# Sharing the last half product of two feed-forwards, folding the layer norm's affine into weights, and a new issue order, in a fused recurrence-and-transformer kernel

## The chip, the core and the metric

The kernel runs on one core of one Trainium2 chip. The metric is device time in microseconds (us) for one execution, smaller is better. The time of a kernel is the median of several runs; a separate profiled execution supplies the trace.

## What is computed

The input `x` has 16 sequences of 512 tokens with 128 channels, all in 32-bit floats. Two branches read the normalised input and meet at the end:

```python
xn = layernorm(x)
s = recurrence(xn)                  # conv of 4 taps, two gates, a scan over time, a projection, an rms norm
t = xn
for l in range(2):                  # two transformer layers
    h = shift_token(t)              # the second 64 channels one token late
    q, k, v = split(h @ wqkv[l])    # 8 heads of 64
    t = t + local_attention(rotary(l2norm(q) * qs[l]), rotary(l2norm(k) * ks[l]), v) @ wo[l]   # windows of 64
    h = layernorm(shift_token(t)) * ln_g[l] + ln_b[l]
    a, g = split(h @ w1[l] + b1[l]) # 341 columns each
    t = t + (a * gelu(g)) @ w2[l] + b2[l]
out = x + s * silu(t)
```

The part that the change is mostly about is the last three lines of the layer: a layer norm with gain and shift, a product to 2 x 341 columns, a gated product, and a product back to 128 channels.

## The kernel before

**Work and tiles.** A sequence is 4 token tiles of 128. Per layer and tile there are three projections (`Q`, `K`, `V`), transposes of queries and keys (`tr`), scores (`sim`), a softmax (`nmA/B`, `exA/B`, `rA/B`, `PA/B`), transposes of the weights (`PT`) and the mix with the values (`PV`); per pair of tiles an output projection (`wo`). Per layer and sequence follow the layer norm and the feed-forward: `tx` transposes the stream to tokens, `bn` and `ag` take mean and variance on VectorE, `pw` raises the variance to -1/2 on GpSimd, `nm` normalises on VectorE, `th` transposes back on TensorE and `hT` copies the result to memory on ScalarE, applying gain and shift there. Then for each of three chunks of 128 columns: `g` and `a` are products on TensorE, `ge` is the GELU on ScalarE, `hi` is `(a + b) * gelu` on VectorE, and `yy` adds the chunk's product with `w2` into one accumulator. `r0` and `r1` add the result to the stream.

**Halves.** Every product with 512 columns of moving data is issued by `matmul` (L599 to L602) as two halves of 64 output columns, one for each half of TensorE's columns, and the profile counts two instructions for each half, so a product is a group "x4" there.

The feed-forward's 341 columns are padded with zeros to 384, which is 3 products for `g` and 3 for `a`, or 12 halves.

**Order.** Nothing decides the order at run time. Each task is a name and an item (a sequence, a tile or a chunk), `PLACES` gives its place in one list of 6176 tasks, `in_order` sorts them, and a loop issues them; every engine runs its own instructions strictly in this order. `OPENED` gives for each task the one of 7 accumulator banks (PSUM) that each of its tiles takes; an eighth bank holds the small norms of the attention. `ROOM` gives the number of buffers of each tile in memory. Set-up work (loads of weights, the decay rate, the rotary tables, the masks) hangs behind a few tasks in a table `behind`; for instance the decay rate, 18 small VectorE instructions, comes right behind the first sequence's statistics:

```python
        ("fbn", 0): [decay_rate], ("c0", 0): [lambda: rotary_table(0, nc.vector)],
```

**Names and lines of the profile that matter below.** L547 and L551 are statistics, L478 to L491 the decay rate, L557 to L561 the power on GpSimd, L567 and L573 the normalisation (first norm and layers' norms), L590 and L597 transposes, L602 every product made by `matmul` (`q`, `k`, `v`, `0g`, `0a`, `0y`, ..., and the taps `cv`), L611 and L613 the two copies that form the shifted stream `xS`, L617 the copy `xp`, L704 and L741 the rotary sum and the normalisation of queries and keys on GpSimd, L816 the exponentials, L830 the softmax's division on GpSimd, L851 the mix, L869 the output projection, L876 its sum, L882 `hT`, L889 the GELU, L893 `hi`, L904 `r0` and `r1`.

Of the kernel before, what the change touches and what calls it, by code (L numbers as in the profile page):

```python
# [17 lines left out]
P = 128  # L18
HEADS = 8
DH = 64  # L20
# [9 lines left out]
BANKS = 7  # L30

ROOM = {
    "0mv": 4, "1mv": 4, "fmv": 3, "g": 2, "gelu": 3, "h": 1, "hT": 2, "hid": 3, "kT": 4, "lx": 1, "max": 8, "ms": 3,
    "nx": 2, "oT": 2, "pT": 2, "pr": 3, "qT": 2, "rot": 4, "s": 4, "sq": 2, "sw": 4, "th": 3, "thi": 2, "thr": 2,
# [4 lines left out]
    "ld": "0 1 8 9 88 90 156 39 1028 170 297 535 460 331 210 576",  # L39
    "fbn": "2 2 13 85 107 45 130 25 1069 135 304 531 465 360 168 612",  # L40
    "fag": "3 3 14 97 97 61 152 49 1034 204 207 601 533 236 156 620",
    "fpw": "5 2 15 100 95 74 139 51 1032 204 208 599 699 97 148 695",
    "fnm": "8 7 26 146 156 42 1026 172 295 533 464 329 212 571 334 181",
    "ftx": "10 16 35 251 48 1006 200 299 436 519 376 205 547 349 192 511",
    "xp": "11 24 49 236 44 1005 203 298 435 522 372 208 547 353 192 506",
    "xs0": "12 19 45 254 40 1002 207 297 431 528 379 207 531 351 191 513",
    "xs1": "16 23 106 461 -181 971 276 376 426 441 426 225 456 362 167 643",
    "c0": "13 52 78 195 30 1018 195 294 434 548 351 203 561 340 193 508",
    "cv": "14 48 38",
    "c1": "21 57 69 216 15 1014 192 295 433 555 348 199 561 340 198 509",  # L50
    "c3": "25 64 68 218 13 1014 195 295 427 557 365 188 562 332 208 520",
    "gr": "42 52 214 143 128 847 263 217 442 536 363 225 528 368 208 499",
    "sr": "52 51 230 130 128 846 260 217 466 517 367 220 530 361 223 482",
    "gi": "74 46 77 221 59 958 182 295 430 553 359 194 559 350 179 530",
    "si": "87 38 91 216 75 933 183 300 429 547 367 189 576 332 181 530",
    "ea": "68 42 243 307 390 414 338 156 793 170 372 625 259 214 549 312",
    "in": "113 17 173 134 151 857 182 303 455 525 359 193 575 333 191 520",
    "a2": "86 62 214 321 376 421 341 152 858 152 314 637 250 276 487 336",
    "m": "155 126 126 319 339 475 319 147 945 65 335 802 52 290 476 333",
    "rt": "255 34 191 453 558 170 440 240 701 15 699 412 361 227 448 459",  # L60
    "u": "282 24 241 399 556 174 446 229 699 10 709 406 372 226 458 438",
    "sc": "294 19 261 420 518 174 478 194 698 40 718 365 376 225 464 453",
    "yo": "301 25 283 390 530 175 515 150 698 166 625 350 355 241 461 487",
    "s2": "307 30 280 403 514 177 514 153 706 154 626 387 319 240 459 489",
    "ms": "310 31 293 390 513 182 508 159 702 157 622 391 316 240 460 494",
    "mp": "314 32 315 367 513 184 507 159 701 157 623 389 320 237 458 496",
    "ss": "329 21 319 378 506 178 508 165 700 149 629 403 301 237 461 495",
    "c2": "371 11 1013 192 296 432 556 361 186 562 340 199 526",
    "Q": "19 10 20 36 29 36 41 27 43 177 87 59 81 89 85 69 131 63 86 54 170 60 136 40 146 107 115 44 118 103 118 67 "
    "97 68 112 58 156 57 125 46 180 88 86 69 83 62 126 31 145 143 115 81 121 79 98 22 106 134 118 47 80 137 101 42 "  # L70
    "-5045 39 80 51 133 42 91 58 139 57 95 82 137 47 150 114 135 49 101 76 160 64 103 39 133 43 102 39 187 55 123 124 "
    "144 50 84 70 119 51 115 62 218 33 96 106 141 50 99 42 189 60 80 60 161 52 93 73 200 5 27 11 99 4 47 39",
    "sqq": "24 10 32 32 30 37 56 32 23 180 74 73 88 78 87 65 132 70 76 55 192 41 133 64 117 127 108 45 136 79 114 62 "
    "105 74 117 42 157 73 111 46 192 78 84 70 100 43 138 22 144 142 108 86 123 83 89 28 115 125 118 42 94 129 99 42 "
    "-5032 38 72 52 128 49 91 53 149 41 93 86 133 72 134 113 132 46 122 60 167 59 102 64 106 45 110 40 185 67 106 126 "
    "140 47 97 60 119 60 120 62 208 31 88 117 139 39 110 39 206 35 90 82 132 67 95 72 194 2 16 21 99 3 49 38",
    "rq1": "30 10 20 32 79 15 18 36 45 164 89 58 90 74 90 64 142 52 99 43 177 57 146 43 134 106 109 47 135 89 123 61 "
    "96 66 125 42 167 56 118 45 181 98 102 44 94 57 123 39 133 152 116 83 119 72 97 31 114 113 116 60 89 116 103 75 "
    "-5079 44 81 46 131 50 86 58 147 58 89 85 135 57 152 116 123 56 96 97 135 61 98 42 133 43 102 43 182 66 117 126 "
    "142 66 98 39 117 51 115 71 208 64 73 98 143 59 86 58 175 78 61 86 140 47 96 82 185 11 27 21 85 5 50 72",  # L80
    "rq2": "27 30 16 48 53 9 24 21 71 147 88 58 89 76 96 65 144 58 84 43 177 58 142 31 150 106 109 52 120 97 133 58 "
    "90 74 105 66 159 51 119 58 191 67 111 43 102 43 138 19 149 153 110 81 126 66 95 27 105 135 115 54 81 131 119 44 "
    "-5063 35 82 66 119 49 89 51 144 61 91 88 134 52 140 132 113 61 96 111 120 62 105 49 120 43 114 29 187 84 93 149 "
    "121 64 80 70 106 64 109 72 201 37 99 108 139 50 95 42 185 77 69 63 154 62 81 82 194 3 35 7 98 6 49 73",
    "addq": "43 24 12 52 53 21 31 133 12 88 106 67 89 49 113 92 84 70 97 116 105 95 86 106 83 93 124 122 70 66 137 "
    "45 99 95 100 140 71 110 68 38 208 70 108 42 115 30 131 29 200 84 113 89 119 83 85 33 176 46 118 57 94 140 92 123 "
    "-5140 39 105 41 124 38 120 24 164 47 111 102 110 144 44 146 101 111 58 95 123 48 122 64 103 30 110 65 161 74 113 "
    "166 98 59 109 65 100 37 150 37 198 83 90 153 64 53 105 38 197 88 32 136 82 67 96 163 88 7 100 -5 40 34 50 91",
    "K": "23 10 23 34 45 24 49 17 40 177 103 53 98 60 109 54 136 52 88 50 184 48 137 38 182 90 94 66 102 101 131 53 "
    "103 73 119 39 179 38 120 65 164 95 80 77 74 78 113 48 125 143 136 66 124 69 95 41 90 136 125 42 79 132 113 33 "  # L90
    "-5037 35 89 51 124 44 82 70 125 63 98 81 137 68 127 109 137 48 110 74 171 47 106 48 120 44 107 50 175 53 121 128 "
    "153 37 85 90 110 41 114 62 219 31 118 105 127 43 99 74 166 51 80 63 158 51 101 68 196 6 52 20 74 22 25 39",
    "sqk": "28 10 37 22 61 21 47 24 36 180 97 45 120 40 114 58 140 45 85 55 186 35 139 58 164 97 80 69 109 92 137 48 "
    "107 72 121 32 186 33 127 69 160 87 86 78 81 76 110 38 145 130 136 68 116 69 98 43 101 132 116 38 81 137 110 31 "
    "-5039 40 95 63 106 43 94 61 139 66 91 64 154 50 137 119 123 63 106 59 183 60 92 49 113 55 102 38 185 59 107 126 "
    "163 32 90 86 106 54 112 64 211 33 124 90 129 55 95 73 161 47 84 79 138 56 102 78 187 11 61 15 63 25 25 29",
    "rk1": "44 7 32 44 41 -4 51 45 17 208 67 67 83 85 87 52 146 42 87 52 188 58 122 41 191 82 92 63 118 90 127 74 95 "
    "69 119 63 145 44 119 77 150 101 72 78 77 77 109 50 158 107 138 80 118 66 97 52 81 136 123 42 87 118 122 29 -5037 "
    "49 70 63 120 59 58 87 119 92 66 80 141 80 102 125 124 49 112 81 217 -5 107 62 100 55 93 58 173 49 135 119 151 74 "
    "49 98 108 52 98 75 201 53 102 124 107 73 82 61 169 69 70 71 142 62 97 65 182 24 49 26 56 20 27 43",  # L100
    "rk2": "37 17 16 53 38 37 22 32 19 182 102 67 87 81 82 59 144 37 101 43 183 61 118 47 179 90 98 60 106 102 128 "
    "63 110 64 110 63 155 46 120 62 155 110 69 79 80 68 113 52 125 139 133 90 119 62 85 57 79 137 119 47 98 112 110 "
    "45 -5046 30 90 62 115 69 64 72 129 64 82 98 130 64 124 110 147 40 106 99 191 3 107 50 126 65 78 61 161 56 115 "
    "138 146 79 58 90 111 48 99 75 217 14 125 107 136 28 99 70 164 72 82 50 152 48 110 69 197 -3 58 23 61 24 28 46",
    "addk": "48 10 35 44 63 11 18 129 16 126 86 42 116 115 51 43 135 31 96 62 171 109 72 108 157 46 100 77 123 96 "
# [174 lines left out]
}  # L280

OPENED = {
    "ftx": "01565121510532425006352661604304",
    "c0": "2431121055464",
    "cv": "202",
    "gr": "3562365444046040",
# [34 lines left out]
def all_tasks(B, NT):  # L321
# [49 lines left out]
    for s in range(B):  # L371
        add(s, ("tf", [*two("tf", s), ("th", s)]), "tn", "z", ("xld", [("x", s)]), "zs", "zx", "ot")
# [676 lines left out]
```

## Time and profile before

| what | value |
|---|---|
| runs | 1306.75, 1307.97 and 1308.43 us; median 1307.97 us |
| the profiled execution's own time | 1309.2 us |
| its span, first to last instruction | 1307.4 us, so 1.8 us lie around it |
| mean granted TensorE clock | 0.993 |
| HBM | 13.05 MB read, 4.19 MB written, 13 GB/s over the span |
| DMA issues | 224 copies `vl<-vs` (2.3 us to landing), 16 each of `xtok`, `x` and `out`, and the weights |
| ScalarE table loads | 74 of 1283 ns |

The page of the profile gives busy times of the engines (PE is TensorE's products, PEld its weight loads, DVE VectorE, ACT ScalarE, POOL GpSimd), the span in 40 slices, and the costliest groups of instructions: line, engine, operation, written and read tile, shapes and count, then busy us and mean ns of one, then the idle time just before and what ended it. Tables by stretch give the busy us of each engine between two times. The ends of products are modelled, so a group's mean duration is longer than the spacing of its instructions.

### The profile page before, as it was taken

How to read it: one execution, taken by the hardware profiler on the slowest of the kernel's cores; microseconds unless marked ns; L12 is line 12 of the kernel's file. 1: busy time of each engine (PE TensorE's matmuls, PEld its weight loads, DVE VectorE, ACT ScalarE, POOL GpSimd, SP SyncE). 2: the span in 40 equal slices, each digit the busy share in tenths (PEclk: the TensorE clock that was granted, in tenths of full speed). 3: DMA queues.
4: the chain of work that ended last, by engine and by line, in shares of the span. 5: the costliest groups of instructions: out<-in, count | busy, mean ns of one | idle time of the engine just before them, and what ended most of it. 6: DMA issues, size and time to landing. Idle time of an engine off the chain costs nothing.

```text
span 1307.4 us, 45281 instructions
## 1 busy us (share of the span) xinstructions
PE 1259.8 (96%) x17688; PEld 701.5 (54%) x17688; DVE 1132.1 (87%) x3024; ACT 1179.1 (90%) x3804; POOL 1040.1 (80%) x1009
## 2 busy tenths in 40 slices
PE   6889999999999999999999999999998999999997
PEld 2455565645555555555555555655455555655463
DVE  7989989988989989988998999879988889858963
ACT  5898999989999998998989999998999899997793
POOL 6987988966988878887877988857797698874782
PEclk9989999999999999999999999999999999999999
DMA  5110121102111202011121101211012011130111
GB/s 178 43 36 20 22 43 30 27 2 58 35 50 39 52 13 50 8 41 43 38 54 30 26 16 37 55 23 38 26 31 47 18 35 34 27 71 2 38 35 45
DMA packets 46773, 49.52 MB, mean 38 GB/s; under 512 B 4704, under 2 KB 31456, under 8 KB 46560
## 3 DMA queue, kind: packets, MB, share of 16 engines
q1 hardware_dynamic: 46560, 46.63, 14.6%
q8 instruction: 140, 2.29, 0.7%
q14 instruction: 73, 0.60, 0.2%
HBM read 13.05 MB, written 4.19 MB: 13 GB/s over the span
## 4 chain that ended last, share of the span: by engine, by line
PE 53%; DVE 19%; ACT 16%; POOL 8%; issue 4%; DMA 0%; POOLq 0%; DVEq 0%; ACTq 0%
ACT pr L816 6%; PE q L602 5%; PE x L869 5%; PE o L851 5%; PE sA L803 5%; PE k L602 5%; PE t L762 4%; PE v L602 3%; PE p L838 3%; DVE xn L573 3%; PE 0y L602 3%; PE 1g L602 3%; PE 0a L602 3%; DVE rot L697 2%; DVE norms L709 2%
## 5 line engine op out<-in xcount | busy, mean ns | idle before, releaser
L704 POOL TENSOR_TENSOR rot<-rot,sw 128x512 f32<-128x512 f32 x256 | 326.9, 1290 | 35.2 <-DVE rot L697 12.2
L830 POOL TENSOR_TENSOR pr<-pr,sum 128x512 f32<-128x512 f32 x256 | 263.7, 1042 | 93.0 <-DVE sum L824 65.3
L741 POOL TENSOR_TENSOR rot<-rot,y 128x1024 f32<-128x1024 f32 x128 | 242.9, 1903 | 38.5 <-DVE y L736 37.1
L816 ACT ACTIVATE pr<-sA,max 128x128 f32<-128x128 f32 x512 | 189.0, 441 | 4.4 <-DVE max L809 3.3
L816 ACT ACTIVATE pr<-sB,max 128x128 f32<-128x128 f32 x512 | 188.6, 442 | 1.4 <-DVE max L809 1.1
L709 DVE TENSOR_REDUCE norms<-sq 128x16 f32<-128x1024 f32 x128 | 155.7, 1217 | 6.1 <-ACT sq L690 4.2
L842 ACT COPY pT<-p 128x512 f32<-128x512 f32 x256 | 143.6, 657 | 14.9 <-PE p L838 14.4
L851 PEld LDWEIGHTS o<-pT,vl 128*64 128x64 f32 x2048 | 111.4, 138 | 49.1 <-issue 29.1
L816 ACT ACTIVATION_READ_ACCUMULATOR pr<-sB,max 128x1 f32 x512 | 137.8, 281 | 0.0
L816 ACT ACTIVATION_READ_ACCUMULATOR pr<-sA,max 128x1 f32 x512 | 137.6, 280 | 0.0
L602 PE MATMUL q<-wqkv,xS 128*64 128x512 f32 x512 | 135.3, 611 | 0.5 <-ACT pr L816 0.2
L803 PE MATMUL sA<-kT,qT 64*64 64x128 f32 x2048 | 134.8, 270 | 0.0
L803 PE MATMUL sB<-kT,qT 64*64 64x128 f32 x2048 | 134.2, 270 | 0.0
L602 PE MATMUL k<-wqkv,xS 128*64 128x512 f32 x512 | 133.7, 604 | 0.5 <-ACT pr L816 0.5
L602 PE MATMUL v<-wqkv,xS 128*64 128x512 f32 x512 | 132.3, 600 | 1.5 <-DVE rot L697 0.6
L851 PE MATMUL o<-pT,vl 128*64 128x64 f32 x2048 | 128.2, 224 | 0.9 <-ACT pr L816 0.5
L851 PE MATMUL o<-pT,vs 128*64 128x64 f32 x2048 | 126.9, 223 | 0.0
L803 PEld LDWEIGHTS sA<-kT,qT 64*64 64x64 f32 x2048 | 121.2, 134 | 8.9 <-issue 0.2
L869 PE MATMUL x<-oT,wo 128*64 128x257 f32 x1024 | 123.1, 382 | 0.0
L803 PEld LDWEIGHTS sB<-kT,qT 64*64 64x64 f32 x2048 | 120.6, 134 | 0.0
L851 PEld LDWEIGHTS o<-pT,vs 128*64 128x64 f32 x2048 | 105.0, 139 | 0.2 <-ACT pT L842 0.2
L809 DVE TENSOR_REDUCE max<-sA 128x4 f32<-128x512 f32 x128 | 87.0, 680 | 16.2 <-PE sB L803 14.6
(155 smaller groups left out, 3218.3 us busy)
## 6 DMA issues: line engine op xcount, KB each, us to landing
vl<-vs SPq DMA_DIRECT2D x224, 128.0 KB, 2.3
xtok<-in_x SPq DMA_DIRECT2D x16, 256.0 KB, 3.1
x<-in_x SPq DMA_DIRECT2D x16, 256.0 KB, 3.4
out<-th SPq DMA_DIRECT2D x16, 256.0 KB, 2.4
wqkv<-in_wqkv SPq DMA_DIRECT2D x2, 768.0 KB, 6.8
w<-in_w SPq DMA_DIRECT2D x2, 384.0 KB, 6.3
rot<-in_rope SPq DMA_DIRECT2D x1, 512.0 KB, 5.8
wo<-in_wo SPq DMA_DIRECT2D x2, 256.0 KB, 5.2
```

Source lines behind the costliest of these rows:

```text
L602: nc.tensor.matmul(ps[col : col + 64], w[:, col : col + 64], v, start=start, stop=stop)
L704: nc.gpsimd.tensor_tensor(r, r, at["sw", *n, "qk"[i]], ALU.add)
L709: nc.vector.tensor_reduce(at["nx", *pair(n)][:, 0, 16 * j : 16 * j + 16], sq, AX.X, ALU.add)
L741: nc.gpsimd.tensor_tensor(flat, flat, bc(at["y", *pair(n)][:, 0, 16 * j : 16 * j + 16], DH), ALU.mult)
L762: nc.tensor.transpose(four(at["bank", f"t{w}", *n])[:, i, p, :], r[rows, i, 2 * p : 2 * p + 2, :], c["ident"][rows, rows])
L803: nc.tensor.matmul(out_(w, par)[:, p, :], q[r, p, half[w]], k[r, p, col : col + P], start=False, stop=p == 3)
L809: nc.vector.tensor_reduce(at["max", *n, h], sim, AX.X, ALU.max, negate=True)
L816: nc.scalar.activation(at["pr", *n][:, g, :], sim[:, p, :], AF.Exp, bias=at["max", *n, h][:, p : p + 1], accum_out=at["sum", *n][:, g : g ...
L830: nc.gpsimd.tensor_tensor(w, w, bc(at["sum", *n][:, g], P), ALU.mult)
L842: nc.scalar.copy(at["pT", *n][:, w], heads(ps))
L851: nc.tensor.matmul(o[64 * par : 64 * par + 64, p, 64 * w : 64 * w + 64], at[("vl", "vs")[w], *n][:, h * DH : (h + 1) * DH], pT[:, w, 4 * p ...
L869: nc.tensor.matmul(ps[64 * r : 64 * r + 64, 0 : 2 * P + 1], w, o[:, k, 1 - r : 2 * P + 2 - r], start=k == 0, stop=k == 3)
```

## The change

1. **Eleven halves.** 341 columns are five halves of 64 and 21 more. The host now puts the last 21 columns of `a` (`LEFT`) into the free columns of the last `g` chunk (columns 64 to 84 of it, beside `g`'s own last 21 at 96 to 116). So the last chunk of `a` is one half of 64 columns, and a second VectorE instruction `hj` multiplies the 21 columns. The last chunk's product with `w2` reads 85 rows instead of 128.
2. **A shared product.** The half of layer 1's sequence `u` and that of layer 0's sequence `u + 2` are issued together as task `ap`, one to each half of the columns, for `u` from 0 to 13. The four others (layer 0's sequences 0 and 1, layer 1's 14 and 15) are issued alone.
3. **Layer norm.** Gain and shift leave `hT`: `ws` scales `w1` in place once for each layer, `wb` and `bb` add `w1`'s product with the shift to the bias `b1`. `hT` becomes a plain copy. `nm` becomes two VectorE instructions over four token tiles that subtract the mean; a new task `nr` on GpSimd multiplies by the inverse deviation.
4. **Stream.** The copy `xs0` moves from ScalarE, where it read the accumulator, to GpSimd, where it reads `xp`.
5. **Order.** The table `behind` is gone: its work consists of tasks with places of their own (`l0`, `l1`, `l2`, `dr0`, `dr`, `t0`, `t1`, `cm`). All places and banks are new (6240 tasks). `hT` has 3 buffers instead of 2 and `th` 2 instead of 3.

```diff
-    "nx": 2, ... "hT": 2, ... "th": 3, ...
+    "nx": 2, ... "hT": 3, ... "th": 2, ...
...
-            add(s, (p + "tx", [...]), (p + "bn", [...]), p + "ag", p + "pw", p + "nm")
+            add(s, (p + "tx", [...]), (p + "bn", [...]), p + "ag", p + "pw", p + "nm", p + "nr")
...
-                add(C, (p + "a", [("bank", p + "a", *C), ("hid", l, *C)]), p + "hi")
+                if c < KCH - 1 or not 0 <= s - 2 * (1 - l) < B - 2:
+                    add(C, (p + "a", [("bank", p + "a", *C)]))
+                add(C, (p + "hi", [("hid", l, *C)]), *[p + "hj"] * (c == KCH - 1))
...
+    for u in range(B - 2):
+        add(u, ("ap", [("bank", "ap", u)]))
...
     def normalised(p, s, src):
         mv, xn = at[p + "mv", s], at["xn" + p, s]
-        for t in range(NT):
...
-                for r, v in enumerate(src):
-                    to = xn[:, t, 64 * r : 64 * r + 64]
-                    nc.vector.tensor_scalar(to, v[:, t], mv[:, t, 0:1], mv[:, t, 2:3], ALU.subtract, ALU.mult)
+        for r, v in enumerate(src):
+            nc.vector.tensor_tensor(xn[:, :, 64 * r : 64 * r + 64], v, bc(mv[:, :, 0], 64), ALU.subtract)
+
+    def unit(p, s):
+        xn = at["xn" + p, s]
+        nc.gpsimd.tensor_tensor(xn, xn, bc(at[p + "mv", s][:, :, 2], D), ALU.mult)
...
     def stream(s, r):
-        if r == 0:
-            for r, ps in enumerate(two("fx", s)):
-                nc.scalar.copy(half_of(at["xS", s][0:64, 0:L], r), half(ps)[0:64])
-        else:
-            nc.gpsimd.tensor_copy(at["xS", s][64:128, 1 : L + 1], at["xp", s][64:128, 3:])
+        rows = slice(64 * r, 64 * r + 64)
+        nc.gpsimd.tensor_copy(at["xS", s][rows, r : r + L], at["xp", s][rows, 3:])
...
-    def affine(s, l):
+    def shift_bias(l, part):
+        ps = at["bank", "wb", l]
+        if part == 0:
+            for i in range(2 * KCH):
+                matmul(ps[:, i : i + 1], c["w1", l][:, i // KCH, i % KCH, :], c["ln_b", l])
+        elif part == 1:
+            nc.vector.tensor_tensor(c["b1", l], ps[:, 0 : 2 * KCH], c["b1", l], ALU.add)
+        else:
+            w1 = c["w1", l].rearrange("p s k m -> p (s k m)")
+            nc.scalar.activation(w1, w1, AF.Copy, scale=c["ln_g", l])
+
+    def keep_h(s, l):
         for r, ps in enumerate(two(f"{l}th", s)):
-            to = half_of(at["hT", l, s], r)
-            nc.scalar.activation(to, half(ps), AF.Identity, bias=c["ln_b", l], scale=c["ln_g", l])
+            nc.scalar.copy(half_of(at["hT", l, s], r), half(ps))
...
+    def last_columns(C, l):
+        nc.tensor.matmul(at["bank", f"{l}a", *C][0:64], c["w1", l][:, 0, C[0], 0:64], at["hT", l, C[1]], start=True, stop=True)
+
+    def last_of_both(u):
+        for l in range(DEPTH):
+            hT = at["hT", l, u + 2 * (1 - l)]
+            nc.tensor.matmul(at["bank", "ap", u][64 * l : 64 * l + 64], c["w1", l][:, 0, KCH - 1, 0:64], hT, start=True, stop=True)
+
     def hidden(C, l):
...
+    def hidden_rest(C, l):
+        to, gate = slice(64, 64 + LEFT), slice(96, 96 + LEFT)
+        b = c["b1", l][to, C[0] : C[0] + 1]
         nc.vector.scalar_tensor_tensor(
-            at["hid", l, *C], at["bank", f"{l}a", *C], b, at["gelu", l, *C], ALU.add, ALU.mult
+            at["hid", l, *C][to], at["bank", f"{l}g", *C][to], b, at["gelu", l, *C][gate], ALU.add, ALU.mult
         )

     def narrow(C, l):
-        matmul(at["bank", f"{l}y", C[1]], c["w2", l][:, C[0], :], at["hid", l, *C], C[0] == 0, C[0] == KCH - 1)
+        rows = slice(0, P if C[0] < KCH - 1 else 64 + LEFT)
+        w, hid = c["w2", l][rows, C[0], :], at["hid", l, *C][rows]
+        matmul(at["bank", f"{l}y", C[1]], w, hid, C[0] == 0, C[0] == KCH - 1)
```

The new list begins `ld` 0, `ld` 1, `fbn` 0, `l0`, `fag` 0, `fbn` 1, `fpw` 0, `fag` 1, `l1`, `fpw` 1, `fnm` 0, `dr0`: the first sequence's aggregation `fag` stands ahead of the decay rate. TensorE's queue begins with the transposes of sequence 0, then those of sequence 1, then the taps `cv` of sequence 0, then `q`, `v` and `k`.

## The prediction

> **What bounds the kernel now.** I read the page first, then busy times by stretch, then the chain that ended last, then groups by shape, then the two ends in order of time.
>
> ```profile
> PE 1259.8 (96%) x17688; PEld 701.5 (54%) x17688; DVE 1132.1 (87%) x3024; ACT 1179.1 (90%) x3804; POOL 1040.1 (80%) x1009
> PE   6889999999999999999999999999998999999997
> PEclk9989999999999999999999999999999999999999
> ```
>
> TensorE is busy throughout; the gaps are in the first three slices and the last. By stretch (us, then busy us of PE, PEld, DVE, ACT, POOL, then clock and DMA):
>
> ```profile
> 0.00:30.00 30.00, 18.17 (x84) 6.27 (x84) 20.48 (x67) 14.86 (x34) 17.55 (x52) 1.00 0.60 191
> 30.00:130.00 100.00, 90.41 (x1182) 49.25 (x1178) 90.91 (x258) 89.28 (x277) 88.07 (x92) 0.95 0.14 34
> 130.00:1200.00 1070.00, 1056.02 (x15180) 595.26 (x15180) 945.73 (x2483) 1001.99 (x3260) 866.76 (x805) 1.00 0.15 34
> 1200.00:1308.00 108.00, 95.18 (x1252) 50.72 (x1248) 74.97 (x221) 72.99 (x238) 67.76 (x63) 0.98 0.15 36
> ```
>
> Busy products have modelled ends, so I check by start spacings, which the chain shows where it runs along TensorE (start, us, group):
>
> ```profile
> 1222.42 1.72 PE 1g L602 x8
> 1227.57 0.86 PE k L602 x4
> 1241.07 0.71 PE t L762 x16
> 1242.36 1.08 PE o L851 x32
> 1279.73 1.85 PE x L869 x16
> ```
>
> A product (x4) takes 0.86 us. There are 384 of Q, K, V, 288 of the feed-forwards, 32 gates and 6 taps: 710 x 0.86 = 611. Per tile and layer two transposes (0.71), the mix (1.08) and the scores (1.21 between neighbours at 610 us), 128 x 3.71 = 475; output projections 64 x 1.85 = 118; small transposes and the recurrence's projection about 54. That is some 1258 us of the 1307: TensorE's own work sets the time, apart from the ends and the stretch 30 to 130, where DVE, ACT and POOL are as full as it is.
>
> The Trainium skill (Perfetto Trace Analysis, Identifying the Most-Contended Engine) speaks against this: product busy time is a bad measure, weight-load busy time the better one. That stands at 54% here; taken alone it would make the saved products worth nothing and the forecast about 1308. The spacings decide for me, since they do not use modelled ends.
>
> **The change part by part.**
>
> ```profile
> L573 DVE TENSOR_SCALAR xn<-0tx,0mv 128x64 f32<-128x64 f32 x128 | 33.7, 335 | 2.9 <-POOL 0mv L558 2.6
> L876 DVE TENSOR_TENSOR xS<-x,xS 128x257 f32<-128x257 f32 x64 | 26.7, 417 | 10.2 <-PE x L869 9.7
> L830 POOL TENSOR_TENSOR pr<-pr,sum 128x512 f32<-128x512 f32 x256 | 263.7, 1042 | 93.0 <-DVE sum L824 65.3 <-PE x L869 12.0 <-ACT pr L816 5.4
> L904 DVE SCALAR_TENSOR_TENSOR xS<-0y,cols,xS 64x512 f32<-64x512 f32 x32 | 23.9, 747 | 10.3 <-PE 0y L602 9.9
> L882 ACT ACTIVATE hT<-0th,cols 128x256 f32<-128x256 f32 x32 | 16.5, 577 | 5.8 <-PE 0th L590 5.8
> L768 ACT COPY qT<-t 128x256 f32<-128x256 f32 x256 | 91.3, 449 | 4.4 <-PE t L762 4.1
> L613 POOL COPY xS<-xp 64x512 f32<-64x512 f32 x16 | 9.9, 617 | 4.9 <-ACT xp L617 4.0
> ```
>
> *Products.* 32 last `a` products become 14 shared pairs and 4 single halves. A pair costs 0.86 if its halves run together and 1.72 if not. The nearest row is L869, whose two halves also read different moving data: 16 instructions of 257 columns in 1.85 is 0.45 ns per column, a product's 4 of 512 in 0.86 is 0.42. So they pair: 0.86. A single half has the same two passes, 0.86; if it took half, four would give 1.7 more. Saved: 32 - 18 = 14, x 0.86 = **-12.0**. The last `y` product reads 85 rows. Its bounds are 0.86 and 1.72 (halves one after the other, +27.5 for 32); every 128-row pair above costs 0.86, and 85 rows do not fit the 64-row form of the scores, so 0.86, no gain.
>
> *Bias.* `wb` adds 48 instructions of one column: between 0 (covered by TensorE's early gaps) and 48 x 0.138 (a bare weight load) = 6.6; nearest is the mix, 1.08/32 = 0.034 each: **+1.6**.
>
> *Other engines*, at nothing while TensorE is the bound. VectorE: `nm` from 2.11 per sequence and layer (eight, below) to two of 0.42, 32 x -1.27 = -41; `hj` 32 x 0.75 = +24 (21 rows cost what 64 do; L904 and the 128-row L893 are equal); net -17. GpSimd: `nr` 32 x 1.04 and `xs0` 16 x 0.62, +43, to 1083, or 84% of 1296. ScalarE: `hT` 64 x -0.12, `xs0` -11.7, `ws` about 2 x 0.95; its order of functions now needs 76 table loads of 1.283 instead of 74; together -15. If TensorE were not the cover, GpSimd's +43 would be the dearest of these.
>
> The Trainium skill (GPSIMD Engine Reference, Engine selection) advises VectorE for two-input elementwise work, GpSimd being about twice as slow. Rows here give 1.04 against some 0.68; by the rule `nr` would cost 1.4, GpSimd +54 in all, still under its idle time.
>
> *Head.* Before, the statistics' aggregation stands behind the decay rate on VectorE:
>
> ```profile
> 7.81 0.37 DVE L551 BATCH_NORM_AGGREGATE fmv<-st 128x2 f32<-128x6 f32 x4
> 10.28 1.65 ACT L567 ACTIVATE xnf<-xtok,fmv 128x128 f32<-128x128 f32 x4 [6.17 <-POOL fmv L561]
> 13.31 3.68 PE L602 MATMUL cv<-xp,squares 128*64 128x512 f32 x8 [0.96 <-ACT xp L617]
> ```
>
> Now it follows the statistics (end at 4.37): 3.44 us earlier, so sequence 0 is normalised from 6.8 to 8.5. But ScalarE then takes the decay rate's two (0.4) and sequence 1 (1.65) before the copy `xp`, at 10.6 to 11.4; the taps start at 11.4 instead of 13.3. `q` then waits for two copies on GpSimd (1.24, to 12.6), under the taps' 3.4. The DMAs keep their order but for `xtok` 1 ahead of the constants; the weights of `q`, issued at 3.7 with 6.8 to landing, are there at 10.5. **-1.9**, between -3.4 and 0 (if the full stretch after it absorbs it). In that stretch (the first 120 us of TensorE's work in either list) VectorE has 4 less, ScalarE 3 less, GpSimd 4 more: 0, between -4 and +4.
>
> *Tail.*
>
> ```profile
> 1285.82 2.11 DVE L573 TENSOR_SCALAR xn<-1tx,1mv 128x64 f32<-128x64 f32 x8 [0.20 <-POOL 1mv L558]
> 1288.06 0.47 PE L590 MATMUL 1th<-squares,xn 64*128 64x64 f32 x8
> ```
>
> The last norm takes power, then 2.11. Now the subtraction needs no power and runs beside it, and 1.04 follows: -1.1. `hj` ahead of the last `y` product gives back up to 0.75, of which earlier `y` products hide some: **-0.6**, between -1.1 and 0.2.
>
> *Banks.* `g` of the last chunk holds its bank until `hj`, a shared product for two readers. In the lists, openings less than 0.9 us of TensorE's work behind the last reader of the same bank go from 43% to 47%: **+1**, between 0 and +5.
>
> Sum: -12.0 + 1.6 - 1.9 - 0.6 + 1 = -11.9. On the profiled execution 1309.2 gives 1297.3; it lies 1.2 above the median, and from 1307.97 the forecast is **1296**. The bounds above give its own range 1290 to 1301.
>
> **Rivals.**
>
> *GpSimd's queue becomes the wait (slower).* `nr` puts GpSimd, which runs strictly in order, between VectorE and each of 32 back-transposes. If every second `nr` finds one rotary sum (1.29, L704) late ahead of it, 16 x 1.29 = 20.6 turn -11.9 into +8.7: 1317. It decides from 11.9/32 = 0.37 us per transpose. For it: GpSimd at 88% in 30 to 130. Against it: 16% idle overall, and the norm's chain itself is 1.1 shorter while TensorE's work between `tx` and `th` of layer 1 shrinks only from 5.4 to 4.7 (medians in the lists).
>
> *The 85-row halves do not pair (slower).* +27.5 - 11.9 = +15.6: 1324. Only the lack of a row speaks for it.
>
> *Half is lost to waits.* `ap` needs two norms of different layers; in a tenth of cases it stands just 0.9 us of work behind the later transpose, about one copy pair. 14 x 0.4 = 5.6 lost: 1302.
>
> *More is gained.* TensorE idles 9.6 us in 30 to 130 and 14 in 130 to 1200. If lighter VectorE and ScalarE take back a third, -8: 1288.
>
> *Nothing arrives.* ScalarE, at 90%, holds TensorE at the old pace: about 1308.
>
> **How the numbers follow.** Chances: forecast 0.56, more gained 0.11, half lost 0.15, nothing 0.04, GpSimd 0.11, halves 0.03. Faster by over 0.2% (2.6 us, what a measurement of this kernel can tell) is 0.56 + 0.11 + 0.15 = 0.82, within it 0.04, slower 0.14. The range 1288 to 1311 leaves out the 85-row case (0.03), most of GpSimd's (0.08) and the lower part of "more gained" (0.05).
>
> **What would show it.** Right: `ap` x56 with 0.86 per four, `y` unchanged in spacing, PE busy down by about 10 at the same share, first taps near 11.4, `nr` near 1.04. Wrong: TensorE waiting for `xn` on POOL at `th` for more than 12 us in all, `y` at twice its spacing, idle in 130 to 1200 well above 14 us, or GpSimd above 90%.

## The result, and the profile after

The kernel after takes **1286.88 us** (median of 4 runs, 1286.74 to 1286.91) against 1308.20 for the kernel before beside it (1306.75 to 1308.53): ratio 0.9839, 95% interval 0.9822 to 0.9856, 21.3 us less. The forecast was 1296, its range ended at 1288: more was gained than it allowed. The profiled execution of after took 1286.86 with a span of 1285.1.

From the page of after, busy times, TensorE's slices and its clock:

```profile
PE 1244.4 (97%) x17672; PEld 697.2 (54%) x17672; DVE 1112.3 (87%) x2866; ACT 1164.9 (91%) x3776; POOL 1081.9 (84%) x1057
PE   7899999999999999999999999999999999999997
PEclk9999999999999999999999999999999999999998
```

VectorE's fall of 20, ScalarE's of 14 and GpSimd's rise of 42 are near those of the prediction (17, 15 and 43); TensorE's busy time fell by 15, where the prediction had about 10. By stretch (us, then busy us of PE, PEld, DVE, ACT, POOL, then clock and DMA):

```profile
0.00:30.00 30.00, 21.41 (x138) 8.59 (x140) 21.43 (x68) 15.61 (x34) 20.48 (x57) 1.00 0.65 204
30.00:130.00 100.00, 91.99 (x1276) 50.82 (x1274) 95.31 (x260) 92.64 (x294) 96.45 (x99) 0.98 0.15 35
130.00:1200.00 1070.00, 1057.26 (x15200) 596.42 (x15198) 941.99 (x2403) 996.11 (x3235) 909.22 (x853) 1.00 0.15 34
```

In 30 to 130 TensorE does 1276 instructions where it did 1182, though VectorE and GpSimd are busier there than before. Its idle time falls only from 9.6 to 8.0 there and from 14.0 to 12.7 in 130 to 1200. The changed groups, by shape:

```profile
L942 PE MATMUL ap<-hT,w 128*64 128x512 f32 x56 | 14.5, 596 | 0.0
L636 PE MATMUL 1y<-hid,w 85*64 85x512 f32 x64 | 16.7, 600 | 0.0
L957 DVE SCALAR_TENSOR_TENSOR hid<-0g,cols,gelu 21x512 f32<-21x512 f32 x16 | 12.0, 748 | 0.4
L603 DVE TENSOR_TENSOR xn<-0tx,0mv 128x256 f32<-128x256 f32 x32 | 12.0, 415 | 0.2
L607 POOL TENSOR_TENSOR xn<-xn,0mv 128x512 f32<-128x512 f32 x16 | 16.8, 1048 | 0.9 <-DVE xn L603 0.2
```

The shared product and the product of 85 rows cost per instruction what a full one costs (598 and 599 ns for `1a` and `0a` before). The subtraction costs 415 ns, `nr` 1048, `hj` 748, all as forecast. The head and the tail in order of time (start, us, group):

```profile
4.38 0.36 DVE L583 BATCH_NORM_AGGREGATE fmv<-st 128x2 f32<-128x6 f32 x4
11.49 3.68 PE L636 MATMUL cv<-xp,squares 128*64 128x512 f32 x8 [0.38 <-ACT xp L648]
28.21 1.51 PE L636 MATMUL wb<-cols,w 128*64 128x1 f32 x48
...
1263.69 1.05 POOL L607 TENSOR_TENSOR xn<-xn,1mv 128x512 f32<-128x512 f32 x1
1265.03 0.46 PE L624 MATMUL 1th<-squares,xn 64*128 64x64 f32 x8
```

**Where the time went.** I add up TensorE's own work at the spacing of its instructions where they follow each other without a wait (a product instruction 0.215 us, a rotary transpose 0.044, one of the mix 0.034, and so on), and read how far the clock time is ahead of that work ("behind", below). The work is 1239.0 us before and 1228.4 after, 10.6 less (forecast 10.4, products and bias). The rest of the 22.3 by which the two spans differ is waiting (the last column is near the end of TensorE's work):

| behind, at so much work done (us) | 5 | 100 | 900 | 950 | the end |
|---|---|---|---|---|---|
| before | 15.7 | 34.3 | 49.1 | 54.4 | 59.1 |
| after | 12.4 | 25.7 | 41.6 | 42.6 | 47.1 |
| gained in between | 3.3 | 5.3 | -1.1 | 4.3 | 0.2 |

So the waits gave 12 where the prediction had 1.5: the head 3.3 (forecast 1.9), the stretch after it 5.3 (forecast 0), and 4.3 in one place near the end. Of the 3.3, up to about 1 is chance: five runs below leave the head of before as it is, and in their traces "behind" at 5 us of work is 0.2 to 1.4 less than in this one. Two of the three places are also those where the clock was halved: before has it in 50.0 to 53.4, 87.5 to 94.4 and 992.1 to 995.5 us, after only in 80.3 to 83.7. TensorE did 6.6 us of work at that pace before and 1.6 after, so at most 5.0 of the 12 lie there.

### The profile page after: what moved, and what is told of

The parts are those of the page before. It is cut to its first block, busy times and chain, and to the rows that moved or that the text cites. A ratio compares the mean times of both kernels' runs of the same rounds, so it can differ in the third digit from the quotient of the medians.

```text
span 1285.1 us, 45136 instructions
## 1 busy us (share of the span) xinstructions
PE 1244.4 (97%) x17672; PEld 697.2 (54%) x17672; DVE 1112.3 (87%) x2866; ACT 1164.9 (91%) x3776; POOL 1081.9 (84%) x1057
## 4 chain that ended last, share of the span: by engine, by line
PE 49%; DVE 18%; ACT 15%; POOL 12%; issue 4%; DMA 0%; POOLq 0%; DVEq 0%; ACTq 0%
ACT pr L847 7%; PE q L636 5%; PE o L882 5%; PE x L900 5%; PE v L636 4%; PE sA L834 4%; PE k L636 4%; POOL rot L735 3%; PE p L869 3%; POOL rot L772 3%; PE t L793 3%; DVE norms L740 3%; DVE max L840 2%; PE 0g L636 2%; POOL pr L861 2%
## 5 line engine op out<-in xcount | busy, mean ns | idle before, releaser
L847 ACT ACTIVATION_READ_ACCUMULATOR pr<-sA,max 128x1 f32 x512 | 134.3, 273 | 0.0
L840 DVE TENSOR_REDUCE max<-sA 128x4 f32<-128x512 f32 x128 | 86.9, 681 | 23.3 <-PE sB L834 16.2
```

What stands on the lines that cost most here:

```text
L840: nc.vector.tensor_reduce(at["max", *n, h], sim, AX.X, ALU.max, negate=True)
L847: nc.scalar.activation(at["pr", *n][:, g, :], sim[:, p, :], AF.Exp, bias=at["max", *n, h][:, p : p + 1], accum_out=at["sum", *n][:, g : g ...
```

## The experiments

The theory on record was TensorE's work plus the ends, with the other engines at nothing. The rivals: the other engines have a price of their own; the head or the half clock makes the rest; the new list does. Differences below are medians against 1286.88 for kernels made from after, and against the runs of before on the same chip for kernels made from before. The medians of before on the five chips of the experiments lie between 1307.5 and 1309.25, and after was timed on one chip only, so a difference to after of under some 2 us is not told apart from none.

### The work and the head

*Each shared pair issued twice*, which puts the 14 saved products back:

```diff
-        for l in range(DEPTH):
+        for l in (0, 1, 0, 1):
```

> The changed kernel with each of the 14 shared pairs of last halves issued twice (the second overwrites the first with the same values). The forecast's term for the shared product is 14 x 0.86 = 12.0 us: if TensorE's work sets the time, 1286.9 becomes 1298.9 (between 1296 and 1302). Rival, TensorE has slack behind other engines in the changed kernel: the time rises by under 6 us.

1300.21, **+13.3** for 12.0 of work. TensorE's work counts in full; nothing hides it.

*The decay rate back ahead of the first aggregation*, in after (`dr0` and `dr` moved to just before `fag` 0):

> The changed kernel with the decay rate's 18 small VectorE instructions put back ahead of the first sequence's aggregation. If the head is worth what I forecast, +1.9 us (1288.8). If the early start also spares TensorE low-clock time after it (theory: head and clock gave the 9.4 us that I missed), +5 to +9 us, with the clock's low stretches before 130 us longer than the 3.4 us of the changed kernel. If neither, under +1.

1291.89, **+5.0**. *The decay rate later*, in before:

```diff
-        ("fbn", 0): [decay_rate],
+        ("fnm", 0): [decay_rate],
```

> The kernel before with one edit: the decay rate issued behind the first sequence's normalisation instead of ahead of its aggregation. Forecast's head term: -1.9 to -3.4 us against before (1308). Theory of head and clock: -5 to -9, with less low-clock time than the 13.7 us of before. Theory that the new list as a whole did it: under 2 us.

1305.22, **-2.7** (0.9963 to 0.9983). In both the difference is there at the first 5 us of work and stays to the end, and the half clock of the old list stays too. The head is worth 2.7 to 5.0, more than 1.9.

### The norm, in either list

*`nr` on VectorE*, in after (`nc.vector` for `nc.gpsimd` at L607):

> The changed kernel with the multiplication by the inverse deviation (nr) on VectorE instead of GpSimd, at the same place: VectorE +32 x 0.68 = +22 us, GpSimd -33 us. If VectorE's relief is what gave the missed 9.4 us, the time rises by 5 us or more. If TensorE's work, the head and the clock explain it, it stays within 2 us of 1286.9. If GpSimd's queue holds the back-transposes, it falls by over 2 us.

1311.13, **+24.2**: all of the change's gain is lost. But VectorE's busy time rises by 35.7 here, not by 22, and GpSimd's falls by 23, not by 33, so this run doesn't give a clean price of VectorE's time. By shape:

```profile
L607 DVE TENSOR_TENSOR xn<-xn,1mv 128x512 f32<-128x512 f32 x16 | 20.5, 1283 | 2.9 <-POOL 1mv L590 2.9
L607 DVE TENSOR_TENSOR xn<-xn,0mv 128x512 f32<-128x512 f32 x16 | 16.0, 999 | 2.7 <-POOL 0mv L590 2.7
```

The same instruction takes between 0.67 and 2.38 us in this run, which is told of at the end.

*The new norm in the old list*: two subtractions and the multiplication right behind them, in place of the eight instructions. Then *the subtractions alone* in the old list, which is the same without the last line:

```diff
+        for r, v in enumerate(src):
+            nc.vector.tensor_tensor(xn[:, :, 64 * r : 64 * r + 64], v, bc(mv[:, :, 0], 64), ALU.subtract)
+        nc.gpsimd.tensor_tensor(xn, xn, bc(mv[:, :, 2], D), ALU.mult)
```

> The kernel before with one edit: the layers' norm as two subtractions on VectorE and one multiplication on GpSimd right behind them (VectorE -41 us, GpSimd +33 us; everything else, the list too, as before). If VectorE's relief and the shorter norm chain gave the missed gain: -4 us or more against 1307.9, and the low-clock stretch at 87.5 to 94.4 us gone or halved (TensorE waits there for the old norm). If the new list did it: within 2 us of 1307.9. If GpSimd's hop costs: slower.

> The kernel before, with the normalisation's eight VectorE instructions per sequence replaced by the two subtractions alone; the multiplication by the inverse deviation is left out, on every engine. VectorE falls by 41 us, to about 1092, and nothing is added to GpSimd (1039). Theory 1, VectorE's time is charged at the 0.55 us per us that the two runs with a doubled load showed in the kernel after: 41 x 0.55 = 22 less, about 1286. Theory 2, relief is worth nothing in a list of places that was laid out for the heavier VectorE, as the run with the new normalisation in the old list suggested: 1308, within 3. Between the two (1295 to 1303): the extra hop to GpSimd took back in that run what the lighter VectorE gave.

1308.91, **+1.3** (1.0001 to 1.0020), and 1296.99, **-10.5** (0.9903 to 0.9936). So 41 us off VectorE come with a gain of 10.5 although TensorE is 96% busy, and the 33 us of the multiplication on GpSimd cost 11.8. Neither end of the second expectation was met.

The two numbers are not the price of busy time alone. Leaving the multiplication out also shortens the norm's own chain, from 2.11 us to 0.83, and with the multiplication in, TensorE waits for it at the transpose `th`. The weight loads of the run with the new norm:

```profile
L592 PEld LDWEIGHTS 0th<-squares,xn 64*128 64x128 f32 x128 | 5.2, 138 | 12.7 <-POOL xn L575 7.9 <-issue 1.6 <-POOL kT L752 0.8
L592 PEld LDWEIGHTS 1th<-squares,xn 64*128 64x128 f32 x128 | 5.2, 138 | 10.0 <-POOL xn L575 7.9 <-issue 1.8 <-POOL fmv L558 0.2
```

That is 15.8 us of waiting for `xn`, against 8.8 in before, none in the run with the subtractions alone, and 6.1 in after. No run separates load from chain here.

These two runs also tell where the norm helps. Both have the tasks of before in the same order, so their traces can be laid beside it product by product. The new norm is 1.0 us ahead at 21 us, where nothing has been changed yet, 4.3 ahead at 134 (100 us of TensorE's work), still 4.3 at 350, 1.2 at 950 as at 1010, and 0.6 at the end. The subtractions alone are 1.3, 5.4, 7.0, 11.1 (11.3 at 1010) and 12.9 ahead. In both, the half clock at 50 to 53 and at 87 to 94 us is gone. So the norm gives 3.3 to 4.1 of the 5.3 that the stretch behind the head gained, and nothing at 950 to 1010 us, where after gained 4.3.

*The multiplication left out of after*:

```diff
-        nc.gpsimd.tensor_tensor(xn, xn, bc(at[p + "mv", s][:, :, 2], D), ALU.mult)
```

> The kernel after, with the multiplication by the inverse deviation (`nr`, 32 x 1.05 us on GpSimd) left out: GpSimd falls by 33.6 us to about 1048, nothing else changes. If GpSimd's time has the price downwards that a load had upwards (0.47): -16, about 1271. If a relief gives half of what a load costs, as on VectorE in the old list (0.26 against 0.69): -8, about 1279. If the new list had hidden this load: 1284 to 1287.

1290.15, **+3.3**: slower without it. What cost 11.8 in the old list costs next to nothing in the new one. In the trace one place, shown below, loses 4.4, and all the rest gives back 1.1.

*The old norm in the new list*, behind `pw`:

```diff
+            i, j = at_[p + "nm", s], at_[p + "pw", s]
+            if i < j:
+                order.insert(j, order.pop(i))
...
+                nc.vector.tensor_scalar(to, v[:, t], mv[:, t, 0:1], mv[:, t, 2:3], ALU.subtract, ALU.mult)
```

> The kernel after, with the old normalisation put back: eight instructions of subtraction and scaling per sequence on VectorE, set right behind the inverse deviation `pw` where `nm` had stood ahead of it, and nothing in the place of `nr`. VectorE +41 us (to about 1153), GpSimd -33 (to about 1049). Theory 1, VectorE's time is charged at 0.55 and GpSimd's is not: +22, about 1309. Theory 2, both are charged alike: (41 - 33) x 0.55 = +4, about 1291. Theory 3, the normalisation has no part in what was gained beyond the forecast: within 3 of 1287.

1384.25, **+97**, far outside all three expectations. VectorE now waits for GpSimd's power in its queue; the groups' last column is the idle time ahead of them:

```profile
L605 DVE TENSOR_SCALAR xn<-1tx,1mv 128x64 f32<-128x64 f32 x128 | 33.7, 336 | 19.8 <-POOL 1mv L590 19.8
L605 DVE TENSOR_SCALAR xn<-0tx,0mv 128x64 f32<-128x64 f32 x128 | 33.7, 336 | 23.7 <-POOL 0mv L590 23.7
```

43.5 us of waiting; the old list had 7.6 for the same instruction (2.9 and 4.7 in its rows) and after has 0.4 for the subtraction. The new list is laid out for a subtraction that needs no power, and doesn't bear one that does. The old norm further back, at the place of `nr`, wasn't run.

### What an added microsecond costs, and what one taken away gives

*Steps issued twice.* On VectorE in either list `ms` and `in`, then in after the two subtractions; in after on GpSimd `a2` and the clearing of `vl`, and on ScalarE `s2` and `sr`. The edit is the same for each, shown for `ms` and for the subtractions:

```diff
+            for _ in range(2):
                 nc.vector.tensor_reduce(ms, tok(at["h", s]), AX.X, ALU.add)
...
-        for r, v in enumerate(src):
+        for r, v in 2 * list(enumerate(src)):
```

*Two steps of VectorE left out* of after, `m` and the taps `c2`:

```diff
+        if i == 2:
+            return
...
-            nc.vector.tensor_scalar(g, g, -1.0, -1.0, ALU.mult, ALU.max)
```

> The changed kernel with two VectorE instructions of the recurrence issued twice for each sequence (the mean square's reduction and the gated input, both read from or written beside accumulators or state, same values): VectorE +32 x 0.68 = +22 us, nothing else. If VectorE's relief is worth its length: +5 us or more. If TensorE's work covers it: under +2 us.

> The changed kernel with both subtractions of each layer norm issued twice (same values): VectorE +32 x 0.76 = +24 us, with the second pair beside the power on GpSimd (1.3 us), so that the norm's chain grows by at most 0.3 us. If VectorE's load as such matters: +5 us or more, as with the reductions issued twice. If only the length of the norm's chain matters, or neither: under +2 us.

> The kernel before, with the reduction `ms` and the product `in` issued twice: VectorE +22 us (to about 1151), nothing else. Theory 1, VectorE's time is charged at 0.55 in either list: +12, about 1320. Theory 2, the old list has no room left on VectorE, so that a load costs nearly its full time: +18 to +22, 1326 to 1330. Theory 3, the old list's waits lie elsewhere and hide it: 1308 to 1312.

> The kernel after, with the square `a2` of each sequence (16 x 1.04) and the clearing of `vl` (32 x 0.52) issued twice on GpSimd: +33 us there (1082 to about 1115), nothing on the other engines. If GpSimd's time is charged as VectorE's is, 0.55 per us: +18, about 1305. If only the chain through VectorE counts: 1287 to 1290. A price of 0.2 would give 1293.

> The kernel after, with ScalarE's square `s2` and its tanh `sr` of each sequence issued twice: 32 x 0.66 = +21 us on ScalarE (1165 to about 1186), nothing elsewhere. If ScalarE's time is charged like VectorE's (0.55 to 0.7): +12 to +15, 1299 to 1302, and the 15 us that the change took off ScalarE could stand for several us of the unexplained gain. If it is hidden beside TensorE: 1287 to 1290.

> The kernel after, with two of VectorE's steps left out: `m`, the negation and bound of `g` (16 x 0.63), and the taps `c2` (13 x 0.75). VectorE falls by 19.8 us to about 1093. By the price of a load (0.55 to 0.65): -11 to -13, 1274 to 1276. By the price of relief in the old list (0.26): -5, about 1282. If the list hid it: 1285 to 1287.

| kernel, engine | its busy time, us | the kernel's time, us | ratio of the two |
|---|---|---|---|
| after, TensorE (pairs twice; work) | +12.0 | +13.3 | 1.1 |
| after, VectorE (`ms`, `in`) | +19.8 | +12.1 | 0.61 |
| after, VectorE (subtractions) | +23.9 | +15.9 | 0.66 |
| before, VectorE (`ms`, `in`) | +19.8 | +15.1 | 0.76 |
| after, ScalarE (`s2`, `sr`) | +19.5 | +10.2 | 0.52 |
| after, GpSimd (`a2`, clearing) | +33.9 | +15.6 | 0.46 |
| before, VectorE (no scaling; shorter chain too) | -41.1 | -10.5 | 0.26 |
| after, VectorE (no `m`, `c2`) | -14.0 | -1.3 (not told apart from 0) | 0.1 or none |
| after, GpSimd (no `nr`) | -32.5 | +3.3 | none |

The five runs of the subtractions issued twice lie between 1298.5 and 1303.0, so that row's ratio is 0.49 to 0.67. The theory that only TensorE counts falls with rows two to six, and the one price for each engine, up and down, with the last three. An added microsecond costs about half or more in the new list, on each engine; in the old list only VectorE was loaded so (0.76), and the norm's multiplication cost 0.36 of its time on GpSimd. A microsecond taken away gives a quarter in the old list, in the one run that tried it, and next to nothing in the new one. In after, VectorE's load by `ms` and `in` pulls "behind" up steadily (by 2.1 at 140 us of work, 5.8 at 500, 10.6 at 900, 12.5 at the end): small waits everywhere, no new bound. It looks as if a list that stands turns a longer instruction into somebody's wait, and a shorter one into idle time unless its followers are moved up.

### The half clock, the stall near the end, and an earlier start

*Products that nobody needs, in three stalls of before*:

```diff
+        if t in (("tr", (0, 2)), ("tr", (0, 3))):
+            for _ in range(2):
+                nc.tensor.matmul(at["bank", "t0", *t[1]][0:64], c["ident"][:, 0:64], c["wqkv", 0][:, 0:INNER])
         do[t[0]](t[1])
+        if t in (("V", (0, 7)), ("sim", (0, 53))):
+            do[t[0]](t[1])
```

> The kernel before, with products that nobody needs put into three stalls of TensorE, at 47 to 49.5 us (two products of 512 columns ahead of each of two rotary transposes), at 84 to 85.5 (one product of `v` issued twice) and at 988 to 990 (one block of scores issued twice), about 0.9 to 1.3 us in each. If the half clock that follows each of these stalls is a loss of its own, its three stretches go and 4 to 6.6 us with them: 1301 to 1304. If it only marks the stall, or another engine is late by then anyway: 1307 to 1310, with the clock at full speed all the same.

1308.48 against 1309.25, ratio 0.9985 to 1.0004. The work done at half clock fell from 6.6 us to 1.7, and the time by at most 2. Product by product, the two traces show why: at the first stall the filler itself holds TensorE up by 1.25 us, then the full clock gives 1.55 back, so the half clock is a loss where it stands; by 70 us other waits have taken what was won (0.5), and at the end the filled kernel is 0.7 ahead. Before's own 64 executions beside the experiments point to a loss too: they took 1306.6 us on average where the mean granted clock was 0.996, 1308.4 at 0.994 and 1310.3 at 0.992. So the half clock costs something in this kernel; how much of the 5.0 us would reach the end stays open.

*The same in the one stall of after*, eight products of 256 columns between the halves of the first sequence's `0tx`:

```diff
+            if t == 2 and to[0] is at.get(("bank", "0tx0", 0)):
+                for _ in range(8):
+                    nc.tensor.matmul(to[0][0:64, 256:512], c["ident"][:, 0:64], c["wqkv", 0][:, 0:256])
```

> The kernel after, with eight products of 256 columns that nobody needs put into TensorE's stall at 77.3 to 79.3 us, between the halves of the first sequence's transposes `0tx`, in the unused half of their bank. If the half clock of 80.3 to 83.7 is a loss of its own: it goes, and 1.6 us with it, 1285.3. If not, or if the filler delays the transposes: 1286.5 to 1287.5.

1287.76, +0.9, not told apart from none. The half clock went, but the filler was twice as long as I had sized it:

```profile
77.11 3.67 PE L631 MATMUL 0tx<-wqkv,squares 128*64 128x256 f32 x16
80.70 0.34 PE L634 MATMUL 0tx<-squares,xS 64*128 64x64 f32 x4
```

The stall had ended at 79.35, so the transposes came 1.35 us late; this run says nothing about the clock alone.

*An earlier first product*, with that filler (`xp` 0 ahead of `fnm` 1, `ftx` 1 behind `cv` 0):

> The kernel after, with the filler of the run before and a changed head: the copy `xp` of the first sequence ahead of the second sequence's normalisation on ScalarE, and the second sequence's transposes `ftx` behind the first taps `cv` on TensorE, so that the first taps start at 9.8 us instead of 11.5. If the start is carried to the end as in the runs of the head: -1 to -1.7 from the head, and the filler's part; 1283.6 to 1286. If the second sequence, 1.7 us later, is missed at once: 1286 to 1288.

1290.80, **+3.9**. The taps start at 9.74, but then ScalarE is late for the third sequence, and the clock halves at 19.8:

```profile
9.74 3.50 PE L639 MATMUL cv<-xp,squares 128*64 128x512 f32 x8 [0.96 <-ACT xp L651]
18.63 1.52 PE L624 MATMUL fx<-squares,xnf 64*128 64x64 f32 x8 [1.41 <-ACT xnf L600]
```

*The scan of sequence 13 one VectorE task later*, in before, where it stands at 987.5 us just ahead of the stall:

> The kernel before with one edit: the scan of sequence 13 stands one VectorE task (rq1 of tile 47, layer 1) later. In the trace of before this scan takes 2.73 us at 987.5 while GpSimd runs beside it, TensorE waits 2.58 us for that rq1, and the clock is low from 992.1 to 995.5 (1.4 us of work at half speed). If that one stall with its clock stretch is the loss that I see there: -3 to -4 us against 1307.9. If the stall only moves on: under -1.

1307.99, no difference (0.9995 to 1.0013). The stall moved with it.

## Why the prediction was wrong

**Right.** The products: 10.6 less work against 10.4, the shared pair and the 85 rows at a full product's spacing, `wb` in 1.51 us against 1.6; put back, the products cost 13.3 against 12.0. The taps at 11.49 against 11.4. TensorE's weight loads waited 6.1 us for `xn` on GpSimd at `th` (5.0 in layer 1), well under the 12 that would have spoken for GpSimd's queue; that rival fell for the new list (in the old list the same norm waits 15.8), and so did the 85-row one.

**Mis-sized.** The head: 3.3 in the trace, 5.0 and 2.7 by the two runs that move the decay rate, where the prediction had 1.9. It had counted the taps' start and not the clock, which reached full speed at 15.5 us instead of 19.3; part of that is chance, as in the five other traces with the head of before it comes at 16.2 to 18.9. The tail's 0.6: `tx` to `th` did shrink, from 5.7 to 4.8, but 0.2 arrived. The bank term of +1 was not measured alone. TensorE's work was put at 1258 us and is 1239.0 by the spacings, so 68 us of the old span were waiting, and not 49. And the range "1290 to 1301" is narrower than its bounds added up: from 1307.97 the products, `wb`, the head with the stretch behind it, the tail and the banks give some 1287.5 to 1311.8.

**The step that failed** is "*Other engines*, at nothing while TensorE is the bound", and with it "0, between -4 and +4" for the stretch from 30 to 130. TensorE busy at 96% doesn't make the others free: in the old list the norm without its multiplication, 41 us off VectorE, gives 10.5, and in the new list an added microsecond costs about half of itself or more on each of the three. In the stretch put at 0, the norm alone gives 3.3 to 4.1 of the 5.3 measured. Of GpSimd's +43, priced at nothing, the norm's 33 did cost next to nothing, but not because TensorE covers them: they cost 11.8 where the list was not laid out for them. The stream's 10 were not tested alone. The rival "more is gained" named a part of the mechanism, a lighter VectorE, and came within 1.1 us, but that nearness is luck: its size, a third of 23.6 us of idle time, didn't hold, since idle time in those stretches fell by 2.8. The gain also lies in work at half clock and in the head.

**What this adds up to.** The norm alone lies between +1.3 (its multiplication paid for, old list) and -10.5 (hidden, as it is in the new list). `hj` puts 24 us on VectorE against it, the stream's copy 10 on GpSimd, and ScalarE has 14 less, a relief that no run priced. Work (-10.6), head (-3.3) and a norm hidden (-10.5) give -24.4, and `hj` at VectorE's ratios of 0.26 to 0.76 gives back 6 to 18: -6 to -18 against -22.3 between the spans. ScalarE's 14 at the one ratio for relief, 0.26, would be 4 more and close the gap at its near end. So these prices neither reach the measured gain clearly nor exclude it. I think that the list, laid out anew, gave a good part, but that is argued: no run has the old steps in a list laid out anew for them, and the one that comes nearest (+97) shows only what an instruction costs that comes ahead of its input. The stretch at 20 to 100 us of work is for the greater part the norm's. Which edit freed the place at 900 to 950 stays open: neither the norm nor the head did it in the old list.

## What to carry to other kernels

In a kernel whose engines are all 80 to 97% busy and whose order is written out, don't price the other engines at nothing: here a load cost about half its time or more, relief gave a quarter at most. Ask for each moved step whether the list was laid out again for it: the same multiplication cost 11.8 us in the old list and next to nothing in the new. Single edits inside a finished list then say little of what they are worth, and leaving a step out can even make it slower. Measure by TensorE's work at its own spacings and by the time the kernel is behind it, at several points; idle time by stretch showed 3 of the 12 us.

## What the hardware showed

**VectorE and GpSimd block each other.** The scan has two inputs in memory and takes 1.21 us where nothing disturbs it. Left out of after, `nr` makes GpSimd do a rotary sum and a normalisation beside the scan at 125.9 us. First the run without `nr`, in order of time, then after at the same place:

```profile
125.89 4.39 DVE L1006 TENSOR_TENSOR_SCAN h<-thr,thi 128x512 f32<-128x512 f32 x1
126.09 1.26 POOL L735 TENSOR_TENSOR rot<-rot,sw 128x512 f32<-128x512 f32 x1
127.31 1.89 POOL L772 TENSOR_TENSOR rot<-rot,y 128x1024 f32<-128x1024 f32 x1
```

```profile
125.97 1.53 DVE L1006 TENSOR_TENSOR_SCAN h<-thr,thi 128x512 f32<-128x512 f32 x1
126.36 0.98 POOL L810 MEMSET vl<- 64x512 f32 x2
```

1.21 + 1.26 + 1.89 = 4.36, what the scan took: it waits for both whole instructions, while beside the last 0.45 us of a softmax's division and two clearings, which read nothing, it takes 1.53. Without `nr`, TensorE then waits 2.7 us for VectorE and the clock halves at 131.0; this kernel is 4.3 us later than after at 140 us of work, 3.3 at the end. After has one scan as long, 4.47 us at 649.1, beside the end of one sum, a second sum and a normalisation. The scan that I moved in before met two sums:

```profile
986.84 4.28 DVE L937 TENSOR_TENSOR_SCAN h<-thr,thi 128x512 f32<-128x512 f32 x1
```

1.21 + 1.26 + 1.26, and a clearing of 0.52 between them, is 4.25; unmoved it took 2.73 beside one sum. The other way round, a rotary sum of before that starts 0.23 us after a scan, at 944.3, takes 2.06 us. The Trainium skill (SBUF — State Buffer, SBUF: two separate sides) states it so: a VectorE instruction with two inputs in that memory and a GpSimd instruction that reads it share one pair of ports, as a lock held for the whole instruction. The sums above agree. `nr` on VectorE, with two such inputs, fits it too: it took 0.68 to 0.69 us wherever GpSimd had nothing beside it, and up to 2.38 us where a GpSimd instruction had just begun; the subtraction, which reads an accumulator, takes 415 ns in after.

**The clock.** It halves for windows of 3.41 us on a fixed grid. In before, after and the two filled kernels a window in which TensorE was busy for 0.37 to 0.52 of the time was followed by one at half clock (0.37, 0.39, 0.48 in before, 0.39 in after, 0.52 in before filled), one of 0.53 or more at full clock was not (0.53 and 0.57 in after, 0.58 in before, 0.56 in before filled, 0.54 and 0.58 in after filled). In other runs the line is not so sharp: windows of 0.57 (GpSimd's steps twice) and 0.58 (scan later) were followed by half clock, and in the run with the old norm in the new list windows of 0.43 to 0.52 were not. What decides between them is not shown. The Trainium skill (TensorE: Matmul & The Clock Gate, Part 1: The HAM clock gate) gives the same window, 3413 ns, running freely, and asks for an idle window; here one that was about half busy was often enough.
